# Cross-attention block on one core: the order of the first four blocks laid out anew, with division behind the values and seven-product projection from block 0

## The chip, the core and the metric

The kernel runs on one core of one Trainium2 chip. The metric is device time in microseconds (us), the median of the runs. One further execution is recorded by the hardware profiler; all durations below come from it. The engines are PE (matmul, with its weight loads shown apart as PEld), DVE (vector), ACT (scalar), POOL (GpSimd) and SP (here it only issues transfers).

## The reference

`x` is (16, 1024, 512), the context (16, 64, 512) and the condition (16, 512), all float32. There are 16 heads of 32 features.

```python
def ada_ln(x, c, W_ss, b_ss):            # layer norm, scale and shift from the condition
    h = (x - mean(x)) / sqrt(var(x) + 1e-5)
    scale, bias = split(silu(c) @ W_ss + b_ss, 2)
    return (1 + scale)[:, None, :] * h + bias[:, None, :]

xq, xkv = ada_ln(x, cond, Wss_q, bss_q), ada_ln(ctx, cond, Wss_kv, bss_kv)
q       = xq @ Wq + bq                   # 16 heads x 32
k, v    = split(xkv @ Wkv + bkv)         # 64 keys per batch element
attn    = softmax(q k^T / sqrt(32))      # over the 64 keys
out     = x + (attn v) @ Wp + bp
```

## The kernel before

The 16 x 1024 rows are worked in 32 blocks `i` of 512 rows, so two blocks belong to one batch element; the context is loaded and turned into keys and values for two batch elements at once. All tiles are float32.

One block goes through these steps, named by the helpers that emit them:

- `load_x`; `q_stats` (DVE, row statistics, L260, four tiles); `q_scale` (reciprocal deviation: two small activations on ACT, then small steps on DVE, or, if called "apart", on POOL); `hidden` (ACT normalises four tiles, L321); `turn` (DVE transposes 32 x 32 squares into `ht`); `move` (sixteen transfers from `ht` into `xt`, L508). After these, `xt` holds the features along the partitions.
- The query projection. Blocks 0 to 4 use `queries(i, o)`: four groups of four matmuls of 512 columns (L542), each copied out of PSUM by ACT (`queried`). Blocks 0 to 3 use weights already multiplied with the scale (`query_weights`), later blocks scaled features (`scale_features`, ACT). From block 5 on, `query_product(i, 1..7)` multiplies in seven products instead of eight (Strassen's way, each product four matmuls of 256 columns, L625). It uses sums of weights (`query_weight_sums`, POOL, once) and of features (`feature_sums`, POOL); PSUM banks 0 and 1 collect the products, `query_seed` copies one bank into the other (ACT), `query_out` (ACT) and `query_added` (DVE, L662) take the results out.
- `scores(i, z)` for the two halves `z` of the keys: sixteen matmuls (L673) into two PSUM pair tiles of their own (`ps_s`). DVE takes a maximum over each pair per 32 rows (L685), ACT copies the pair to SBUF (L694). A "crossed" order is maximum 0, copy 1, maximum 1, copy 0; readers of the same tile follow one another. `maxima` merges the two halves and spreads them (DVE, L716), `subtract` takes them off (POOL, L729, two steps; on DVE for block 0), `weights` is the exponential (ACT, L735).
- The softmax denominator goes one of two ways. Blocks 0 to 2 use `sums` (DVE, both halves), `inverse`, and `divide` (POOL, two steps on the 128 x 2048 weights) before `mix`, and `mixed` copies the result out. From block 3 on the division stands behind the values: `total` adds the two halves (POOL, L768), `row_total` sums the rows (DVE), `inverse_rows` takes the reciprocal and sends it through DRAM into another layout (five transfers on SP), `spread_rows` spreads it (DVE), and `divided` multiplies it with the result of `mix` (DVE, L805) on its way out of PSUM.
- `mix` multiplies the weights with the values (L825), into the two pair tiles, or for block 0 into four banks.
- The output projection. Blocks 0 and 1 use `project(i, t)`: four groups of four matmuls of 512 columns (L852), an addition and a transfer out each. From block 2 on `product(i, 1..7)` (L933) does it in seven products, with `weight_sums` (POOL, once), `row_sums` (POOL, two calls of two steps), `biased` (ACT writes the bias into banks 2 and 3), and `added` (DVE, L947). In the `project` way the bias is added to the residual rows beforehand (`residual`, POOL).

The kernel has a manual schedule: each engine carries out its instructions in the order in which the calls stand in the program, and waits at an instruction whose operands aren't ready; what stands behind it waits too. All transfers are issued from SP in this order; a transfer on that queue waits for the eighth before it. PSUM holds the two pair tiles and four single banks, which `bank` hands out in a ring. Blocks 0 to 3 (with the setup: scale and shift rows, biases, `b_v`, `b_p`, weights) have an order written out call by call. From block 4 on a loop over `i` interleaves block `i`'s scores and weights with the projection of blocks `i - 1` and `i - 2`, the queries of `i + 1`, and the way in of `i + 2` to `i + 5`; a tail ends the last two blocks. The call order of a stretch of the way in, for instance, is

```python
    scores(1, 0)
    queries(2, 0)
    q_stats(3)
    queries(2, 1)
    q_scale(3)
    scores(1, 1)
    maxima(1)
    subtract(1)
```

Of the kernel before, what the change touches and what calls it, by code (L numbers as in the profile page):

```python
# [11 lines left out]
ALU = mybir.AluOpType  # L12
# [8 lines left out]
def cross_attention_block(  # L21
# [16 lines left out]
):  # L38

# [99 lines left out]
    def load_x(i):  # L139
        t = xpool.tile([P, NT, H], F32, tag="x", name=f"x_{i}")  # L140
        nc.sync.dma_start(t, rows_of(x, i))
        x_tiles[i] = t
# [34 lines left out]
    for c in range(NC):  # L177
        nc.sync.dma_start(
            b_v_sb[c * 32 : (c + 1) * 32, :],
            b_kv[H + c * P : H + (c + 1) * P].rearrange("(o h) -> o h", o=1).to_broadcast([32, P]),  # L180
        )
# [123 lines left out]
    def q_scale(i, kvb=None):  # L305
        n = NT if kvb is None else NT + 1
        q_rstd[i] = rstd_of(q_mv.pop(i)[:, :n, :], n, "q", i > 1)
        if kvb is not None:
            kv_rstd[kvb] = (q_rstd[i], NT)
# [180 lines left out]
    def turn(i, ts):  # L490

        if ts[0] == 0:
            ht_tiles[i] = hpool.tile([P, 4, NC, NT, 32], F32, tag="ht", name=f"ht_{i}")
        for t in ts:
            nc.vector.transpose(
                ht_tiles[i][:, :, :, t, :].rearrange("p k c b -> p c k b"),
                x_tiles[i][:, t, :].rearrange("p (c k b) -> p c k b", c=NC, k=4),
            )
        if ts[-1] == NT - 1:
            x_tiles.pop(i)  # L500

    def move(i):

        ht = ht_tiles.pop(i)
        xt = qpool.tile([P, 4, NC, NT * 32], F32, tag="xt", name=f"xt_{i}")
        for k in range(4):
            for g in range(4):
                nc.sync.dma_start(  # L508
                    xt[32 * k : 32 * k + 32, g],
                    ht[32 * g : 32 * g + 32, k].rearrange("p c t b -> p c (t b)"),  # L510
                )
        xt_tiles[i] = xt
# [20 lines left out]
    def queries(i, o, later=False):  # L533
        xt, b = xt_tiles[i], i // BPB
        w = wq_tiles.get(b, w_q_sb)
        if o == 0:

            tag = "vb" if i in (1, 3) else "qt"
            qt_tiles[i] = qpool.tile([P, NC, TB], F32, tag=tag, name=f"qt_{i}", bufs=1)
# [13 lines left out]
    def queried(i, o):  # L553
        pq, b = pq_tiles.pop((i, o)), i // BPB
        dst = qt_tiles[i][:, o, :]
# [194 lines left out]
    def inverse(i):  # L750

        v = small.tile([P, HPC * NJ], F32, tag="v", name=f"v_{i}")
        both(v, l_tiles.pop(i), ALU.add)
        nc.vector.reciprocal(v, v)
        vb_tiles[i] = spread(i, v, f"vb_{i}", other=i in (1, NB - 1))
# [9 lines left out]
    def total(i):  # L765

        t = big.tile([P, HPC, TB], F32, tag=f"big{(i + 1) % 2 * 2}", name=f"sum_{i}")
        nc.gpsimd.tensor_tensor(t, s_tiles[i, 0], s_tiles[i, 1], ALU.add)  # L768
        sum_tiles[i] = t

    def row_total(i):
# [7 lines left out]
        )  # L779

# [187 lines left out]
    query_bias_rows()  # L968
    kv_stats(0)
# [10 lines left out]
    load_x(2)  # L980
    load_residual(0)
    load_projection_bias()
# [3 lines left out]
    move(1)  # L986
    load_projection()
    load_x(3)
# [8 lines left out]
    hidden(2, range(NT))  # L997


    scores(0, 0)  # L1000
    turn(2, range(NT))
    move(2)
    load_context(2)
    load_x(4)
    load_residual(1)
    residual(0)
    value_products(0)
    scores(0, 1)
    maxima(0)
    subtract(0, nc.vector, (0,))  # L1010
    value_tiles(0)
    subtract(0, nc.vector, (1,))
    queries(1, 0)
    query_weights(1)
    queries(1, 1)
    weights(0, 0)
    queries(1, 2)
    weights(0, 1)
    sums(0, 0)
    queries(1, 3)  # L1020
    query_weight_sums()
    sums(0, 1)
    inverse(0)
    divide(0)
    scores(1, 0)
    queries(2, 0)
    q_stats(3)
    queries(2, 1)
    q_scale(3)
    scores(1, 1)  # L1030
    maxima(1)
    subtract(1)
    queries(2, 2)
    hidden(3, (0, 1))
    mix(0, apart=False)
    mixed(0)
    hidden(3, (2, 3))
    queries(2, 3)
    turn(3, range(NT))
    move(3)  # L1040
    kv_stats(2)
    q_stats(4)
    project(0, 0)
    weights(1, 0)
    sums(1, 0)
    project(0, 1)
    weights(1, 1)
    residual(1)


    load_x(5)
    q_scale(4)
    kv_scale(2)
    scores(2, 0)
    sums(1, 1)
    inverse(1)
    divide(1)
    project(0, 2)
    context_hidden(2)
    hidden(4, (0, 1))  # L1060
    scores(2, 1)
    maxima(2)
    subtract(2)
    weight_sums()
    hidden(4, (2, 3))
    project(0, 3)
    queries(3, 0)
    queries(3, 1)
    queries(3, 2)
    turn(4, range(NT))  # L1070
    load_residual(2)
    move(4)
    mix(1)
    mixed(1)
    q_stats(5)
    weights(2, 0)
    queries(3, 3)
    project(1, 0)
    sums(2, 0)
    weights(2, 1)  # L1080
    project(1, 1)
    sums(2, 1)
    inverse(2)
    divide(2)
    q_scale(5)
    context_features(2)
    scale_features(4)
    project(1, 2)


    load_x(6)
    scores(3, 0, crossed=True)
    project(1, 3)
    ring[:] = [0, 1]
    scores(3, 1)
    maxima(3)
    subtract(3)
    queries(4, 0)
    load_residual(3)
    hidden(5, (0, 1))  # L1100
    biased(2, 2)
    mix(2)
    mixed(2)
    hidden(5, (2, 3))
    q_stats(6)
    turn(5, range(NT))
    move(5)
    q_scale(6)
    row_sums(2, 0)
    load_x(7)  # L1110
    queries(4, 1)
    product(2, 1)
    added(2, 1)
    product(2, 2)
    weights(3, 0)
    added(2, 2)
    biased(2, 3)
    weights(3, 1)
    total(3)
    queries(4, 2)  # L1120
    keys(2)
    hidden(6, range(NT))
    scale_features(5)
    row_sums(2, 1)
    turn(6, range(NT))
    load_x(8)
    product(2, 7)
    q_stats(7)
    value_products(2)
# [3 lines left out]
    queries(4, 3)  # L1133
    feature_sums(5)
    move(6)
# [198 lines left out]
```

## Time and profile before

| | |
|---|---|
| median of 3 runs | 1057.75 us (1057.16 to 1058.77) |
| profiled execution, its own time | 1058.86 us |
| its span (first to last instruction) | 1057.1 us |
| mean clock granted to PE | 0.998 |
| HBM read / written | 78.85 MB / 34.44 MB |
| page's chain that ended last | PE 80%, DVE 5%, POOL 5%, DMA 4% |

In rows of the page, a group of instructions has the line, the engine, the operation, output and inputs with their shapes, the number of instructions, then "busy us, mean ns of one", and "idle before", the time in which the engine stood still just before them, with what ended it. In a timeline, each row is a run of equal instructions: start, length from the first start to the last end, engine, line and shapes; square brackets hold an idle time ahead of it and what ended that. Busy time is an average over stages with different limits, so the way in is read from timelines and stretches and not from the shares.

### The profile page before, as it was taken

How to read it: one execution, taken by the hardware profiler on the slowest of the kernel's cores; microseconds unless marked ns; L12 is line 12 of the kernel's file. 1: busy time of each engine (PE TensorE's matmuls, PEld its weight loads, DVE VectorE, ACT ScalarE, POOL GpSimd, SP SyncE). 2: the span in 40 equal slices, each digit the busy share in tenths (PEclk: the TensorE clock that was granted, in tenths of full speed). 3: DMA queues.
4: the chain of work that ended last, by engine and by line, in shares of the span. 5: the costliest groups of instructions: out<-in, count | busy, mean ns of one | idle time of the engine just before them, and what ended most of it. 6: DMA issues, size and time to landing. Idle time of an engine off the chain costs nothing.

```text
span 1057.1 us, 22537 instructions
## 1 busy us (share of the span) xinstructions
PE 1033.6 (98%) x8914; PEld 733.7 (69%) x8914; DVE 854.7 (81%) x1134; ACT 618.0 (58%) x951; POOL 752.7 (71%) x470
## 2 busy tenths in 40 slices
PE   6999998999999999999999999999999999999998
PEld 4534365777777787777787787777777777777433
DVE  5698648987789877888878878898778887776993
ACT  3566665665575655667556666566566765565330
POOL 0258794889768869788668986688886886787340
PEclk9999999999999999999999999999999999999999
DMA  9743444444535344544345443444454443334202
GB/s 337 248 127 111 130 122 127 155 150 147 161 94 162 123 140 145 171 148 127 106 131 164 153 158 112 126 141 150 139 157 134 152 134 116 98 115 162 82 30 90
DMA packets 99976, 147.27 MB, mean 139 GB/s; under 512 B 29944, under 2 KB 30096, under 8 KB 99872
## 3 DMA queue, kind: packets, MB, share of 16 engines
q1 hardware_dynamic: 99872, 145.85, 43.5%
q8 instruction: 70, 1.15, 0.5%
q14 instruction: 34, 0.28, 0.1%
HBM read 78.85 MB, written 34.44 MB: 107 GB/s over the span
## 4 chain that ended last, share of the span: by engine, by line
PE 80%; DVE 5%; POOL 5%; DMA 4%; SPq 2%; issue 2%; ACT 1%; POOLq 0%; DVEq 0%; ACTq 0%
PE pp L933 28%; PE pq L625 27%; PE po L825 6%; PE ps L673 6%; PE pp L852 5%; PE pq L542 3%; SPq L508 2%; PE pv L431 2%; PE pk L395 2%; POOL s L760 2%; DMA wss_kv<-in_L_xcond_Wss_kv_dram 2%; DMA b_p_sb<-in_L_xcond_bp_dram 1%; POOL s L729 1%; DMA x<-in_x_dram 1%; DVE s L729 1%
## 5 line engine op out<-in xcount | busy, mean ns | idle before, releaser
L729 POOL TENSOR_TENSOR s<-s,mb 128x2048 f32<-128x2048 f32 x58 | 263.1, 4560 | 160.8 <-DVE mb L716 160.8
L694 ACT COPY s<-ps 128x1024 f32<-128x1024 f32 x128 | 129.5, 1012 | 119.7 <-DVE m L685 82.9
L685 DVE TRANSPOSE_TENSOR_REDUCE m<-ps 128x32 f32<-128x1024 f32 x128 | 150.6, 1214 | 27.1 <-PE ps L673 27.1
L655 ACT ACTIVATE qt<-pq,bias_t 128x256 f32<-128x256 f32 x208 | 85.8, 463 | 110.9 <-PE pq L625 110.9
L933 PE MATMUL pp<-w_p_sb,ot 128*128 128x256 f32 x648 | 148.7, 379 | 0.0
L735 ACT ACTIVATE s<-s 128x2048 f32<-128x2048 f32 x64 | 122.3, 1911 | 42.4 <-POOL s L729 31.8
L947 DVE TENSOR_TENSOR r<-pp,r 128x512 f32<-128x512 f32 x189 | 122.5, 670 | 25.5 <-PE pp L933 19.8
L933 PEld LDWEIGHTS pp<-w_p_sb,ot 128*128 128x128 f32 x648 | 123.4, 190 | 17.4 <-issue 0.7
L768 POOL TENSOR_TENSOR sum<-s,s 128x2048 f32<-128x2048 f32 x27 | 122.7, 4543 | 0.8 <-ACT s L735 0.8
L933 PEld LDWEIGHTS pp<-WT,s 128*128 128x128 f32 x432 | 78.9, 192 | 54.0 <-issue 29.3
L933 PE MATMUL pp<-WT,s 128*128 128x256 f32 x432 | 109.3, 397 | 0.0
L933 PE MATMUL pp<-WT,ot 128*128 128x256 f32 x432 | 102.2, 380 | 0.0
L625 PE MATMUL pq<-xt_sums,wq_sums 128*128 128x256 f32 x416 | 101.0, 386 | 0.0
L321 ACT ACTIVATE x<-x,rstdq 128x512 f32<-128x512 f32 x128 | 96.7, 807 | 4.8 <-POOL rstdq L285 3.2
L625 PE MATMUL pq<-xt,wq_sums 128*128 128x256 f32 x416 | 99.0, 381 | 0.0
L625 PEld LDWEIGHTS pq<-xt_sums,wq_sums 128*128 128x128 f32 x416 | 77.0, 190 | 31.1 <-issue 21.8
L625 PE MATMUL pq<-xt,w_q_sb 128*128 128x256 f32 x416 | 98.4, 380 | 0.1
L260 DVE BATCH_NORM_STATS2 bs<-x 128x6 f32<-128x512 f32 x128 | 86.9, 679 | 5.0 <-DMA x<-in_x_dram 5.0
L662 DVE TENSOR_TENSOR qt<-pq,qt 128x256 f32<-128x256 f32 x104 | 39.1, 418 | 63.1 <-PE pq L625 62.5
L933 PEld LDWEIGHTS pp<-WT,ot 128*128 128x128 f32 x432 | 82.2, 190 | 11.0
L565 ACT ACTIVATE xt<-xt,ss_q 128x512 f32<-128x512 f32 x112 | 84.7, 810 | 6.1 <-DMA xt<-ht 4.3
L625 PEld LDWEIGHTS pq<-xt,w_q_sb 128*128 128x128 f32 x416 | 79.1, 190 | 11.0 <-PE pp L933 0.4
(139 smaller groups left out, 1725.0 us busy)
## 6 DMA issues: line engine op xcount, KB each, us to landing
x<-in_x_dram SPq DMA_DIRECT2D x32, 1024.0 KB, 6.4
r<-in_x_dram SPq DMA_DIRECT2D x32, 1024.0 KB, 5.5
xt<-ht SPq DMA_DIRECT2D x496, 64.0 KB, 2.0
out_dram<-r SPq DMA_DIRECT2D x54, 512.0 KB, 3.8
out_dram<-r SPq DMA_DIRECT2D x20, 256.0 KB, 2.0
wss_q<-in_L_xcond_Wss_q_dram SPq DMA_DIRECT2D x2, 1024.0 KB, 8.8
ctx<-in_ctx_dram SPq DMA_DIRECT2D x8, 256.0 KB, 3.2
wss_kv<-in_L_xcond_Wss_kv_dram SPq DMA_DIRECT2D x2, 1024.0 KB
```

The costliest lines, as they stand in the source:

```text
L260: nc.vector.bn_stats(bs, r)
L321: nc.scalar.activation(dst, src, AF.Identity, bias=rstd[:, 1, j : j + 1], scale=rstd[:, 0, j : j + 1])
L565: nc.scalar.activation(xt[:, :, c, :], xt[:, :, c, :], AF.Identity, scale=ss["q"][:, c, b : b + 1], bias=ss["q"][:, NC + c, b : b + 1],)
L625: nc.tensor.matmul(qa[k][:, m * HT : (m + 1) * HT].rearrange("p (g n) -> p g n", g=2), lhsT=a[:, c, m * P : (m + 1) * P], rhs=x[:, :, c, : ...
L655: nc.scalar.activation(dst, src, AF.Identity, bias=bq_t[:, o : o + 1])
L685: nc.vector.tensor_reduce(m_tiles[i][:, z, 2 * e : 2 * e + 2, :], pss[e].rearrange("p r (j a) -> p r j a", a=32), AX.X, ALU.max, apply_tra ...
L694: nc.scalar.copy(s_sb[:, 2 * e : 2 * e + 2, :], pss[e])
L729: eng.tensor_tensor(s_tiles[i, z], s_tiles[i, z], mb_tiles[i], ALU.subtract)
L735: nc.scalar.activation(p, p, AF.Exp, scale=SCALE)
L768: nc.gpsimd.tensor_tensor(t, s_tiles[i, 0], s_tiles[i, 1], ALU.add)
L933: nc.tensor.matmul(acc[k][:, t * HO : (t + 1) * HO], lhsT=rows[:, c, t * P : (t + 1) * P], rhs=cols[:, c, :], start=n == 2 and t == 0 and ...
L947: nc.vector.tensor_add(r, acc[k].rearrange("p (t h) -> p t h", t=2), r)
```

## The change

Only the order of blocks 0 to 3 and the helpers below change; the loop from block 4 on and the tail are call for call the same.

- Blocks 0 to 2 divide behind the values. Blocks 0 and 2 do it as later blocks do (`total`, `row_total`); block 1 keeps its two `sums` and merges them in the new `halves_total`. The tile of block 0's total lies in the "ot" buffer.
- Blocks 0 and 1 use the seven products for the projection, block 4 for its queries. The residual's bias steps for these blocks go; `biased` takes their place.
- The whole order of blocks 0 to 3 is written anew, with crossed scores throughout.
- `move` issues half of its sixteen transfers from POOL for blocks 1, 2, 3 and 5.
- Large loads are issued at other places: `x` of block 2 ahead of the value bias; `w_p`, `b_p` and the residual rows of block 0 later; `x` of block 3 goes into a residual buffer, `ht` of block 2 into a buffer of the weights.
- `q_scale(2)` does its small steps on DVE.

The helpers:

```diff
     def load_x(i):
-        t = xpool.tile([P, NT, H], F32, tag="x", name=f"x_{i}")
+        t = xpool.tile([P, NT, H], F32, tag="r" if i == 3 else "x", name=f"x_{i}")
         nc.sync.dma_start(t, rows_of(x, i))
         x_tiles[i] = t
...
     nc.sync.dma_start(w_kv_sb, w_kv.rearrange("(c p) o -> p c o", p=P))
     b_v_sb = const.tile([P, P], F32, name="b_v_sb")
-    for c in range(NC):
-        nc.sync.dma_start(
-            b_v_sb[c * 32 : (c + 1) * 32, :],
-            b_kv[H + c * P : H + (c + 1) * P].rearrange("(o h) -> o h", o=1).to_broadcast([32, P]),
-        )
+    def load_value_bias():
+        for c in range(NC):
+            b = b_kv[H + c * P : H + (c + 1) * P].rearrange("(o h) -> o h", o=1)
+            nc.sync.dma_start(b_v_sb[c * 32 : (c + 1) * 32, :], b.to_broadcast([32, P]))
...
     def q_scale(i, kvb=None):
         n = NT if kvb is None else NT + 1
-        q_rstd[i] = rstd_of(q_mv.pop(i)[:, :n, :], n, "q", i > 1)
+        q_rstd[i] = rstd_of(q_mv.pop(i)[:, :n, :], n, "q", i > 2)
...
     def turn(i, ts):
         if ts[0] == 0:
-            ht_tiles[i] = hpool.tile([P, 4, NC, NT, 32], F32, tag="ht", name=f"ht_{i}")
+            pool, tag = (big, "big2") if i == 2 else (hpool, "ht")
+            ht_tiles[i] = pool.tile([P, 4, NC, NT, 32], F32, tag=tag, name=f"ht_{i}")
...
         xt = qpool.tile([P, 4, NC, NT * 32], F32, tag="xt", name=f"xt_{i}")
         for k in range(4):
             for g in range(4):
-                nc.sync.dma_start(
+                (nc.gpsimd if i in (1, 2, 3, 5) and k % 2 else nc.sync).dma_start(
                     xt[32 * k : 32 * k + 32, g],
                     ht[32 * g : 32 * g + 32, k].rearrange("p c t b -> p c (t b)"),
                 )
...
     def queries(i, o, later=False):
         xt, b = xt_tiles[i], i // BPB
         w = wq_tiles.get(b, w_q_sb)
-        if o == 0:
-            tag = "vb" if i in (1, 3) else "qt"
-            qt_tiles[i] = qpool.tile([P, NC, TB], F32, tag=tag, name=f"qt_{i}", bufs=1)
         pq = bank(f"pq_{i}_{o}")
         for c in range(NC):
             nc.tensor.matmul(
...
     def queried(i, o):
         pq, b = pq_tiles.pop((i, o)), i // BPB
+        if o == 0:
+            tag = "vb" if i == 1 else "qt"
+            qt_tiles[i] = qpool.tile([P, NC, TB], F32, tag=tag, name=f"qt_{i}", bufs=1)
...
         v = small.tile([P, HPC * NJ], F32, tag="v", name=f"v_{i}")
         both(v, l_tiles.pop(i), ALU.add)
         nc.vector.reciprocal(v, v)
-        vb_tiles[i] = spread(i, v, f"vb_{i}", other=i in (1, NB - 1))
+        vb_tiles[i] = spread(i, v, f"vb_{i}", other=i == NB - 1)
...
     def total(i):
-        t = big.tile([P, HPC, TB], F32, tag=f"big{(i + 1) % 2 * 2}", name=f"sum_{i}")
+        if i == 0:
+            t = opool.tile([P, HPC, TB], F32, tag="ot", name="sum_0")
+        else:
+            t = big.tile([P, HPC, TB], F32, tag=f"big{(i + 1) % 2 * 2}", name=f"sum_{i}")
         nc.gpsimd.tensor_tensor(t, s_tiles[i, 0], s_tiles[i, 1], ALU.add)
         sum_tiles[i] = t
...
+    def halves_total(i):
+        lt_tiles[i] = small.tile([P, HPC, NJ], F32, tag="lt", name=f"lt_{i}")
+        both(lt_tiles[i].rearrange("p r j -> p (r j)"), l_tiles.pop(i), ALU.add)
```

The order, from the first queries to the loop (`+` new, `-` before):

```diff
     first_features((3,))
     query_weights(0)
     query_bias_rows()
+    load_x(2)
+    load_value_bias()
     kv_stats(0)
     kv_scale(0)
     queries(0, 0, later=True)
...
     hidden(1, (0, 1))
     queries(0, 1)
     hidden(1, (2, 3))
-    load_x(2)
-    load_residual(0)
-    load_projection_bias()
     for h in range(2):
         scale_shift_rows("kv", h)
     turn(1, range(NT))
     move(1)
+    load_x(3)
     load_projection()
-    load_x(3)
+    load_projection_bias()
     queries(0, 2)
     for h in range(2):
         scale_shift("kv", 2 * NC, h)
...
     queries(0, 3)
     keys(0)
     hidden(2, range(NT))
-    scores(0, 0)
     turn(2, range(NT))
     move(2)
+    load_x(4)
+    load_residual(0)
     load_context(2)
-    load_x(4)
-    load_residual(1)
-    residual(0)
     value_products(0)
+    value_tiles(0)
+    scores(0, 0, crossed=True)
+    q_stats(3, (0, 1, 2))
+    queries(1, 0)
     scores(0, 1)
     maxima(0)
-    subtract(0, nc.vector, (0,))
-    value_tiles(0)
-    subtract(0, nc.vector, (1,))
-    queries(1, 0)
+    subtract(0, nc.vector)
+    queries(1, 1)
     query_weights(1)
-    queries(1, 1)
+    weight_sums()
+    queries(1, 2)
     weights(0, 0)
-    queries(1, 2)
+    q_stats(3, (3,))
+    q_scale(3)
+    queries(1, 3)
     weights(0, 1)
-    sums(0, 0)
-    queries(1, 3)
-    query_weight_sums()
-    sums(0, 1)
-    inverse(0)
-    divide(0)
-    scores(1, 0)
+    total(0)
+    ring[:] = [0, 1]
+    scores(1, 0, crossed=True)
+    hidden(3, (0, 1))
     queries(2, 0)
-    q_stats(3)
-    queries(2, 1)
-    q_scale(3)
+    hidden(3, (2, 3))
+    turn(3, range(NT))
+    move(3)
+    row_total(0)
+    inverse_rows(0)
+    load_x(5)
+    load_residual(1)
     scores(1, 1)
     maxima(1)
     subtract(1)
+    queries(2, 1)
     queries(2, 2)
-    hidden(3, (0, 1))
-    mix(0, apart=False)
-    mixed(0)
-    hidden(3, (2, 3))
+    biased(0, 2)
+    mix(0)
+    spread_rows(0)
+    divided(0)
     queries(2, 3)
-    turn(3, range(NT))
-    move(3)
-    kv_stats(2)
-    q_stats(4)
-    project(0, 0)
     weights(1, 0)
+    queries(3, 0, later=True)
+    row_sums(0, 0)
+    q_stats(4, (0, 1))
     sums(1, 0)
-    project(0, 1)
+    q_stats(4, (2, 3), kvb=2)
     weights(1, 1)
-    residual(1)
-    load_x(5)
-    q_scale(4)
-    kv_scale(2)
-    scores(2, 0)
-    sums(1, 1)
-    inverse(1)
-    divide(1)
-    project(0, 2)
-    context_hidden(2)
+    product(0, 1)
+    added(0, 1)
+    product(0, 2)
+    added(0, 2)
+    row_sums(0, 1)
+    q_scale(4, kvb=2)
+    query_weight_sums()
+    biased(0, 3)
+    scores(2, 0, crossed=True)
+    queries(3, 1, later=True)
+    scores(2, 1)
     hidden(4, (0, 1))
-    scores(2, 1)
+    queried(3, 0)
+    hidden(4, (2, 3))
+    queried(3, 1)
     maxima(2)
     subtract(2)
-    weight_sums()
-    hidden(4, (2, 3))
-    project(0, 3)
-    queries(3, 0)
-    queries(3, 1)
+    product(0, 7)
+    added(0, 7)
+    product(0, 6)
+    added(0, 6)
     queries(3, 2)
+    sums(1, 1)
+    halves_total(1)
+    inverse_rows(1)
+    product(0, 5)
+    added(0, 5)
     turn(4, range(NT))
+    move(4)
+    load_x(6)
+    product(0, 4)
+    added(0, 4)
+    product(0, 3)
+    added(0, 3)
     load_residual(2)
-    move(4)
+    weights(2, 0)
+    biased(1, 2)
     mix(1)
-    mixed(1)
     q_stats(5)
-    weights(2, 0)
+    spread_rows(1)
+    divided(1)
+    context_hidden(2)
     queries(3, 3)
-    project(1, 0)
-    sums(2, 0)
+    q_scale(5)
     weights(2, 1)
-    project(1, 1)
-    sums(2, 1)
-    inverse(2)
-    divide(2)
-    q_scale(5)
+    total(2)
+    row_sums(1, 0)
     context_features(2)
+    product(1, 1)
+    added(1, 1)
+    product(1, 2)
+    added(1, 2)
+    row_sums(1, 1)
+    biased(1, 3)
+    row_total(2)
+    inverse_rows(2)
     scale_features(4)
-    project(1, 2)
-    load_x(6)
     scores(3, 0, crossed=True)
-    project(1, 3)
-    ring[:] = [0, 1]
+    feature_sums(4)
+    product(1, 7)
+    product(1, 6)
+    added(1, 7)
+    added(1, 6)
     scores(3, 1)
+    hidden(5, (0, 1, 2))
     maxima(3)
     subtract(3)
-    queries(4, 0)
+    query_product(4, 1)
+    query_seed(4)
+    product(1, 5)
+    added(1, 5)
+    query_product(4, 2)
+    query_out(4, 2)
+    product(1, 4)
+    product(1, 3)
+    hidden(5, (3,))
+    spread_rows(2)
+    added(1, 4)
+    added(1, 3)
+    biased(2, 2)
     load_residual(3)
-    hidden(5, (0, 1))
-    biased(2, 2)
     mix(2)
-    mixed(2)
-    hidden(5, (2, 3))
-    q_stats(6)
+    divided(2)
+    row_sums(2, 0)
     turn(5, range(NT))
     move(5)
-    q_scale(6)
-    row_sums(2, 0)
     load_x(7)
-    queries(4, 1)
+    query_product(4, 6)
+    weights(3, 0)
+    query_out(4, 6)
     product(2, 1)
+    q_stats(6, (0, 1))
     added(2, 1)
     product(2, 2)
-    weights(3, 0)
+    q_stats(6, (2, 3))
     added(2, 2)
-    biased(2, 3)
+    q_scale(6)
     weights(3, 1)
     total(3)
-    queries(4, 2)
-    keys(2)
+    query_product(4, 7)
+    query_out(4, 7)
+    biased(2, 3)
+    row_sums(2, 1)
+    key_products(2, spare("pk_2"))
     hidden(6, range(NT))
+    query_product(4, 5)
+    query_added(4, 5)
+    key_tiles(2)
+    query_product(4, 4)
+    query_added(4, 4)
     scale_features(5)
-    row_sums(2, 1)
     turn(6, range(NT))
     load_x(8)
-    product(2, 7)
-    q_stats(7)
-    value_products(2)
+    value_products(2, spare("pv_2"))
     value_tiles(2)
     row_total(3)
     inverse_rows(3)
-    queries(4, 3)
+    query_product(4, 3)
+    query_out(4, 3)
     feature_sums(5)
+    product(2, 7)
+    q_stats(7)
     move(6)
     q_scale(7)
```

## Prediction

> **What bounds the kernel now.** I read the page's busy shares first, then the stretches around the way in (blocks 0 to 3, written out by hand) and the first turn of the loop (block 4).
>
> ```profile
> PE 1033.6 (98%) x8914; PEld 733.7 (69%) x8914; DVE 854.7 (81%) x1134; ACT 618.0 (58%) x951; POOL 752.7 (71%) x470
> 165.00:170.00 5.00, 2.83 (x12) 1.85 (x11) 4.95 (x7) 2.32 (x7) 2.46 (x6) 1.00 0.15 50
> 170.00:175.00 5.00, 4.16 (x39) 2.71 (x40) 4.42 (x5) 2.83 (x4) 0.00 (x0) 0.68 0.23 46
> ```
>
> The columns of the last two are the stretch, its length, busy time of PE, PEld, DVE, ACT, POOL, then PE's granted clock and DMA. PE is the bound; the one hole with a lower clock (0.68) lies in block 4. PE's timeline there, and at the projections:
>
> ```profile
> 82.60 7.03 PE L852 MATMUL pp<-w_p_sb,ot 128*128 128x512 f32 x16
> 89.56 1.14 PE L673 MATMUL ps<-qt,kt 32*32 32x512 f32 x32
> 142.27 3.62 PE L933 MATMUL pp<-w_p_sb,ot 128*128 128x256 f32 x16
> 161.96 1.98 PE L673 MATMUL ps<-qt,kt 32*32 32x512 f32 x32
> 165.94 1.97 PE L625 MATMUL pq<-xt,w_q_sb 128*128 128x256 f32 x8
> 170.84 1.25 PE L673 MATMUL ps<-qt,kt 32*32 32x512 f32 x32 [2.94 <-ACT s L694]
> 172.02 3.56 PE L933 MATMUL pp<-WT,s 128*128 128x256 f32 x8
> 175.42 1.89 PE L933 MATMUL pp<-w_p_sb,ot 128*128 128x256 f32 x8
> 196.98 1.14 PE L673 MATMUL ps<-qt,kt 32*32 32x512 f32 x32
> 226.61 1.14 PE L673 MATMUL ps<-qt,kt 32*32 32x512 f32 x32
> ```
>
> The first number is the start. Eight fp32 matmuls of 512 columns (a quarter of a block's projection) go start to start in 3.44 to 3.64, eight of 256 (a product) in 1.73 to 1.83. Block 4 takes 196.98 - 161.96 = 35.0; block 5 takes 29.6, 0.4 of them context transposes. So block 4 loses 5.8: an idle of 2.94, a product at half speed after it (3.40 start to start for 1.73), and small waits. The other prices:
>
> ```profile
> L729 POOL TENSOR_TENSOR s<-s,mb 128x2048 f32<-128x2048 f32 x58 | 263.1, 4560 | 160.8 <-DVE mb L716 160.8
> L694 ACT COPY s<-ps 128x1024 f32<-128x1024 f32 x128 | 129.5, 1012 | 119.7 <-DVE m L685 82.9
> L735 ACT ACTIVATE s<-s 128x2048 f32<-128x2048 f32 x64 | 122.3, 1911 | 42.4 <-POOL s L729 31.8
> L768 POOL TENSOR_TENSOR sum<-s,s 128x2048 f32<-128x2048 f32 x27 | 122.7, 4543 | 0.8 <-ACT s L735 0.8
> xt<-ht SPq DMA_DIRECT2D x496, 64.0 KB, 2.0
> ```
>
> The last says that each of a block's sixteen transfers into xt lands 2.0 after its issue; the trace gives 0.51/0.59/2.00 (least, median, most) for the issue itself.
>
> **Removed: work.** Eight projections (from 82.60, 90.63, 95.34, 115.08, 122.39 and 126.98) take 28.2 on PE; fourteen products take 14 x 1.75 = 24.5: -3.7. Block 4's four query groups (3.63 + 3.54 + 3.43 + 3.63 = 14.2) become seven products (12.3): -2.0. Together -5.7. POOL and DVE lose divisions and second row sums (block 0 alone: 9.0 on POOL, 4.5 on DVE) and gain a total (4.5), half sums (5.1) and a division (2.4); neither sets the end by its sum.
>
> **Removed: waits.** From 18.1 to 161.96 PE loses 0.78 (keys' tile), 0.97 (xt of block 1), 1.09 and 0.35 (scores of block 1), 1.93 (mix of block 0, which fills four banks), 0.60, 0.43 and 0.3: 6.4. Block 4 loses 5.8. If nothing new waited, the change would gain 5.7 + 6.4 + 5.8 = 17.9.
>
> **Added: waits.** The new order of each engine is walked with the rows' durations. ACT's fixed costs: a query copy 0.67, a chain of row statistics 1.15, a hidden tile 0.73. DVE's: a maximum 1.2, a spread 2.31, statistics 0.8 a tile. PE's own walk, in starts: values 38.7, scores(0,0) 42.4, queries(1,0) 43.4, scores(0,1) 47.1, three query groups 48.15 to 58.55; scores(1,0) 60.3, queries(2,0) 61.4, scores(1,1) 65.0, two groups 66.1 to 73.2, mix(0) to 76.45, two groups to 83.4, two products, scores(2,0) and queries(3,1) to 91.65; scores(2,1) 93.2, two products to 97.75; queries(3,2) 99.25, three products, mix(1) 108.1, queries(3,3) 110.4, transposes to 114.4; two products from 115.75, scores(3,0) to 120.35; product(1,7) 124.85. From there the steps follow with the waits below to scores(4,0) at 165.85. What PE waits for:
> - scores(1,0) for the last query copy of block 1. It stands on ACT behind q_scale(3), which needs the fourth tile's statistics, and DVE has these behind both subtractions: maxima (from 48.15) 2.35, merge 0.3, spread 2.3, subtractions 4.6, statistics 0.8, so 58.5; ACT then 1.15 and 0.67, 60.3. PE comes at 58.55. Wait 1.75.
> - mix(0) needs the score banks, whose maxima stand behind row_total(0) on DVE: ends 76.45, 0.95 late.
> - scores(2,1): DVE does five statistics tiles, a row sum, two additions and a maximum after divided(0), and ACT a bias copy and two copies: banks free 10.2 after it (93.2), PE there at 91.65. Wait 1.55.
> - queries(3,2): bank 0 is held until the copy of queries(3,0), on ACT behind four hidden tiles' first half and the copies of scores(2,1): 99.25 against 97.75. Wait 1.5.
> - product(1,1): divided(1) stands on DVE behind q_stats(5) (3.2) and spread_rows(1) (2.3): 115.75 against 114.4. Wait 1.35.
> - product(1,7): row_sums(1,0) stands on POOL behind total(2), that needs weights(2,1), that stands on ACT behind q_scale(5) and the last query copy of block 3. From the end of queries(3,3): 0.1 + 0.67 + 1.15 + 1.9 + 4.55 + 2.6 = 11.0; PE has 6.5 of work and waiting until then. Wait 4.5, the largest.
> - query_product(4,2): its seed copy stands on ACT behind the copies of scores(3,1) and three hidden tiles, 6.9 after the scores start; PE comes at 4.6. Wait 2.3.
> - scores(4,1): statistics of block 7 (3.2) stand on DVE ahead of the maxima, behind values' tiles, row_total(3) and reciprocal. Counting from the end of the values: banks free at 10.1, PE there at 8.05. Wait 2.05.
>
> These make 15.95. Nothing is charged for steps that are moved under cover: query_weight_sums (four by 1.27) now stands on POOL ahead of subtract(2), done at 97.1 where the spread for it ends at 98.8, so 1.7 of cover; weight_sums falls into POOL's idle stretch near 46 to 52; the four halves of added() are DVE steps of 0.65 counted above. Then the clock: in the trace a hole of 2.94 is followed by 3.4 at half speed, a loss of 1.67. The wait of 4.5 is longer, so I add 1.7; the two near 2 get nothing, since the trace's holes of 0.9 and less cost nothing (between: 0 to 1.7 each, nearer the small ones in place of work; kept for the range). Sum 17.65.
>
> [...]
>
> **Added: moves on two queues.** Half of the transfers into xt of blocks 1, 2, 3 and 5 are issued from POOL, which issues none now. Bounds for one: 0.2 (POOL's smallest instruction, L283) and 2.0 (SP's slowest). I take SP's median row, 0.6, the same transfer. Up to about 1.0 it costs nothing: block 1's last must issue by 41.4 (turned at 31.2, so 1.28 each); block 3's by 77.9 (turned at 68.6: 1.17) and before subtract(1) at 76.3 (0.96); block 5's ahead of q_scale(6) (1.0). On SP a transfer waits for the eighth before it, so large loads now stand behind moves: xt of block 1 is there near 41.2 instead of 46.5. That wait is among the 6.4. x of block 3 takes a free residual buffer, issued near 37, landing 6.4 later (43.4), before DVE reads it at 45.75 (2.3 of cover). w_p, b_p and r_0 come later than now, but well before weight_sums (46) and added(0,1) (89). The row transfers of inverse_rows(0) stand on SP behind eight moves to 73.7, and land at 78.2; DVE waits for them, 1.9 behind its spread for block 1, and this is in the walk: mix(0) and two query groups keep PE at work until 83.4, divided(0) ends at 83.0.
>
> [...]
>
> **Sum.** 1058.86 (profiled execution; span 1057.1 and 1.8 around it) - 5.7 - 6.4 - 5.8 + 17.65 = 1058.6. The profiled execution lies 1.1 above the median of the runs, so the median becomes 1057.5. The walk itself gives scores(4,1) at 172.4, where before has 170.84 and then 1.67 of clock, 172.5: the two ways agree. Behind block 4 the orders are equal. About 0.2% (2.1 us) is what a measurement can tell from no change.
>
> **Rivals.**
> *Same* (0.36): gain and new waits cancel, 1057.5.
> *Faster* (0.32): the waits for score banks and for what follows the copies (1.55, 1.5, 2.3, 2.05) each count one copy of 1.01 on ACT that may already be done when the maximum ends: -4.0, so 1053.4. For it: in the loop the first copy of a crossed pair starts with the maximum. Against: copies wait 82.9 for maxima over the kernel. If the clock does not drop either, 1051.8.
> *Slower* (0.32): the issue on POOL. A block has eight of these in a row, so at 1.35 each block 1 is 0.55 late, block 3 1.45, block 5 1.9 (2.8 less what PE waits for anyway), +3.9, so 1061.4. It decides from about 1.2 on. At 2.0 it would be 5.8, 6.7 and 7: 1077. For it: one engine must do both issue and arithmetic. Against: SP's same transfers at 0.6.
> That the products are not fewer is no rival: the new PE order shows them.
>
> **Range.** From 1051.8 (the faster case without the clock's drop) to 1063.8 (1.45 each on POOL: 0.8 more in each of three blocks than at 1.35). The likeliest case's own range is 1055.4 to 1059.6. The chances: faster by over 0.2% 0.32, within 0.36, slower 0.32.
>
> **What would show it.** Right: PE idle of some 4 to 5 before the third product of block 1, and PEclk under 1 there; no such hole left in block 4 (a wait of 2); scores(4,0) starting near 165.9 where it starts at 161.96 now, and scores(5,0) at 197 in both. POOL's DMA rows under 1.0. Wrong: scores(5,0) before 194 or after 200; a wait of PE on xt; a hole in PE that is not in the list.

## The result and the profile after

| | before | after |
|---|---|---|
| median, 11 runs each | 1058.11 us (1056.57 to 1060.41) | 1062.20 us (1060.36 to 1065.70) |
| ratio | | 1.0037, 95% interval 1.0025 to 1.0049 |
| profiled execution (span) | 1058.86 (1057.1) | 1060.41 (1058.2) |

The kernel became slower by 4.1 us, where no change was forecast. In the listing after, product is L945, scores L677, query products L629, the copies of scores L698, `subtract` L733, `total` L776 and the moves L512; in the later versions lines stand a few further down. The page's busy shares, then stretches with the columns of the prediction (PEclk is the last but two):

```profile
PE 1028.0 (97%) x8986; PEld 745.8 (70%) x8986; DVE 862.9 (82%) x1150; ACT 613.0 (58%) x944; POOL 754.6 (71%) x494
125.00:130.00 5.00, 3.43 (x10) 2.79 (x11) 4.47 (x5) 2.60 (x3) 4.84 (x5) 0.74 0.83 303
170.00:175.00 5.00, 3.63 (x24) 2.85 (x31) 3.95 (x7) 3.14 (x8) 1.85 (x5) 1.00 0.18 35
```

PE is busy for 5.6 us less (4.6 of it ahead of block 5's first scores, 1.0 behind them, where the orders are equal), and the span is longer all the same. The stretch with a lowered clock has moved from block 4 (0.68 at 170) to the third product of block 1 (0.74 at 125). PE's timeline (start, length, engine and line, in brackets the idle time ahead) shows every wait that the prediction listed:

```profile
61.07 1.13 PE L677 MATMUL ps<-qt,kt 32*32 32x512 f32 x26 [0.85 <-ACT qt L564]
73.90 3.19 PE L837 MATMUL po<-s,vt 32*32 32x512 f32 x64
...
94.31 1.47 PE L677 MATMUL ps<-qt,kt 32*32 32x512 f32 x32 [2.01 <-ACT s L698]
...
100.98 3.70 PE L542 MATMUL pq<-xt,wq 128*128 128x512 f32 x8 [1.55 <-ACT qt L564]
...
117.63 3.72 PE L945 MATMUL pp<-w_p_sb,ot 128*128 128x256 f32 x16 [1.42 <-DVE ot L817]
...
126.57 2.99 PE L945 MATMUL pp<-WT,ot 128*128 128x256 f32 x8 [4.15 <-POOL ot L921]
129.35 2.62 PE L945 MATMUL pp<-WT,s 128*128 128x256 f32 x8
131.91 1.14 PE L677 MATMUL ps<-qt,kt 32*32 32x512 f32 x32
...
139.18 1.99 PE L629 MATMUL pq<-xt,w_q_sb 128*128 128x256 f32 x8 [2.48 <-ACT pq L641]
...
168.56 1.22 PE L677 MATMUL ps<-qt,kt 32*32 32x512 f32 x32
174.80 1.46 PE L677 MATMUL ps<-qt,kt 32*32 32x512 f32 x32 [1.37 <-ACT s L698]
199.59 1.14 PE L677 MATMUL ps<-qt,kt 32*32 32x512 f32 x32
```

The first scores of block 5 start at 199.59 where they started at 196.98. From there the orders are equal, and the difference shrinks to 1.3 by 976, in steps of 0.1 to 0.5 in single blocks: one execution against one other is no more exact than that. The wait of 4.15 is as the prediction had it. POOL's timeline there:

```profile
119.41 4.54 POOL L776 TENSOR_TENSOR sum<-s,s 128x2048 f32<-128x2048 f32 x1 [0.86 <-ACT s L739]
123.89 1.28 POOL L920 TENSOR_TENSOR s<-ot 128x512 f32<-128x512 f32 x1
125.25 1.27 POOL L921 TENSOR_TENSOR ot<-ot 128x512 f32<-128x512 f32 x1
```

The rows that product (1,7) needs were divided on DVE by 118.7 (116.35 and 2.36):

```profile
116.35 2.36 DVE L817 TENSOR_TENSOR ot<-po,vb 128x1024 f32<-128x1024 f32 x2
```

POOL takes them up at 123.89, behind the total of block 2.

The runs also list the clock granted over the whole span. One stretch of half speed costs 1.7 of 1058, which is 0.0016 of it, so 0.998 stands for one, 0.997 for two, 0.995 for three. The profiles, read in stretches of 2 us, bear this out: the clock that they lose is 1.7 us here, and 3.4, 5.1 and 11.9 in other versions, which is one, two, three and seven such stretches. Of 21 runs of the kernel before, beside four of the experiments, 19 have 0.998, one 0.999, one 1.000 (beside the last two, on another chip, five of eleven have 1.000, so how often it comes differs). Of the 11 after, three have 0.998, four 0.997, four 0.992 to 0.995. The three at 0.998 took 1060.36 to 1060.94; the 19 before at 0.998 have a median of 1058.19. So of the 4.1, about 2.2 is there at equal clock, and 1.8 goes with further half speed, which the profiled execution happened not to have.

### The profile page after: what moved, and what is told of

Its sections match the earlier page's. It is cut to its first block, busy times and chain, and to the rows that moved or that the text cites. A ratio compares the mean times of both kernels' runs of the same rounds, so it can differ in the third digit from the quotient of the medians.

```text
span 1058.2 us, 22778 instructions
## 1 busy us (share of the span) xinstructions
PE 1028.0 (97%) x8986; PEld 745.8 (70%) x8986; DVE 862.9 (82%) x1150; ACT 613.0 (58%) x944; POOL 754.6 (71%) x494
## 4 chain that ended last, share of the span: by engine, by line
PE 85%; DVE 6%; ACT 3%; DMA 3%; POOL 2%; issue 1%; SPq 0%; ACTq 0%; DVEq 0%; POOLq 0%
PE pp L945 32%; PE pq L629 30%; PE po L837 6%; PE ps L677 6%; PE pp L864 3%; PE pv L434 3%; PE pq L542 3%; PE pk L398 3%; DMA wss_kv<-in_L_xcond_Wss_kv_dram 2%; DVE m L689 2%; DVE s L733 1%; POOL sum L776 1%; DVE bs L263 1%; ACT s L698 1%; DVE lt L781 1%
## 5 line engine op out<-in xcount | busy, mean ns | idle before, releaser
L733 POOL TENSOR_TENSOR s<-s,mb 128x2048 f32<-128x2048 f32 x58 | 263.1, 4560 | 164.2 <-DVE mb L720 161.0
L698 ACT COPY s<-ps 128x1024 f32<-128x1024 f32 x128 | 129.2, 1012 | 114.9 <-DVE m L689 77.3
L945 PE MATMUL pp<-w_p_sb,ot 128*128 128x256 f32 x696 | 159.8, 379 | 1.4 <-DVE ot L817 1.4
L959 DVE TENSOR_TENSOR r<-pp,r 128x512 f32<-128x512 f32 x203 | 131.9, 670 | 32.5 <-PE pp L945 25.0
L945 PEld LDWEIGHTS pp<-w_p_sb,ot 128*128 128x128 f32 x696 | 132.2, 190 | 20.4 <-DVE ot L817 1.7
L776 POOL TENSOR_TENSOR sum<-s,s 128x2048 f32<-128x2048 f32 x29 | 131.7, 4541 | 3.1 <-ACT s L739 3.1
L945 PEld LDWEIGHTS pp<-WT,s 128*128 128x128 f32 x464 | 84.4, 191 | 55.3 <-issue 30.4
L945 PE MATMUL pp<-WT,s 128*128 128x256 f32 x464 | 116.0, 393 | 0.0
L945 PE MATMUL pp<-WT,ot 128*128 128x256 f32 x464 | 110.8, 382 | 4.2 <-POOL ot L921 4.2
L629 PE MATMUL pq<-xt_sums,wq_sums 128*128 128x256 f32 x432 | 104.9, 386 | 0.0
L629 PE MATMUL pq<-xt,w_q_sb 128*128 128x256 f32 x432 | 102.3, 379 | 2.5 <-ACT pq L641 2.5
L629 PE MATMUL pq<-xt,wq_sums 128*128 128x256 f32 x432 | 102.8, 381 | 0.0
L629 PEld LDWEIGHTS pq<-xt_sums,wq_sums 128*128 128x128 f32 x432 | 79.8, 190 | 32.4 <-issue 22.6
L945 PEld LDWEIGHTS pp<-WT,ot 128*128 128x128 f32 x464 | 88.5, 191 | 18.0 <-POOL ot L921 5.1
L629 PEld LDWEIGHTS pq<-xt,w_q_sb 128*128 128x128 f32 x432 | 81.9, 190 | 14.8 <-ACT pq L641 2.9
L629 PEld LDWEIGHTS pq<-xt,wq_sums 128*128 128x128 f32 x432 | 80.5, 190 | 11.5 <-issue 1.2
```

Source lines behind the costliest of these rows:

```text
L629: nc.tensor.matmul(qa[k][:, m * HT : (m + 1) * HT].rearrange("p (g n) -> p g n", g=2), lhsT=a[:, c, m * P : (m + 1) * P], rhs=x[:, :, c, : ...
L698: nc.scalar.copy(s_sb[:, 2 * e : 2 * e + 2, :], pss[e])
L733: eng.tensor_tensor(s_tiles[i, z], s_tiles[i, z], mb_tiles[i], ALU.subtract)
L945: nc.tensor.matmul(acc[k][:, t * HO : (t + 1) * HO], lhsT=rows[:, c, t * P : (t + 1) * P], rhs=cols[:, c, :], start=n == 2 and t == 0 and ...
L959: nc.vector.tensor_add(r, acc[k].rearrange("p (t h) -> p t h", t=2), r)
```

## The experiments

Two theories were set against each other: the waits of the new order gave the gain back (the prediction's walk), or the loss came from elsewhere (POOL's transfers, the chip's clock). The runs come from three chips, each with runs of the kernel before beside them: a median of 1058.15 before for the first two experiments below, the moves on SP and the first version with the waits taken up; 1058.28 for the four matmuls and the second such version; 1057.57 for the last two. Between chips the ratios are compared.

**The largest wait.** One engine is exchanged:

```diff
-    total(2)
+    total(2, nc.vector)
```

> One edit on the changed kernel: the total of block 2 is added on DVE (about 2.3 us there) and not on POOL (4.54). Theory 1 (the waits that the new order adds give the gain back, the largest of them 4.15 us ahead of the third product of block 1, with 1.8 us of half clock behind it, because row_sums(1,0) stands behind total(2) on POOL): that hole goes, a wait of about 2 for the banks of scores(3,0) appears, because row_total(2) still stands ahead of the maxima, scores(4,0) starts near 164.0 where it starts at 168.56, and the median falls by 4 to 5 us, to 0.9995 of the kernel before. Theory 2 (the 4 us more come from elsewhere, from POOL's transfers or from the later part): the median stays within 1 us of the changed kernel's, 1.003 to 1.004.

Measured: 1058.72 us, ratio 1.0011 (1.0002 to 1.0020), 3.5 us under the changed kernel. PE's timeline:

```profile
125.00 1.97 PE L945 MATMUL pp<-WT,ot 128*128 128x256 f32 x8 [1.68 <-ACT pp L908]
...
166.43 1.22 PE L677 MATMUL ps<-qt,kt 32*32 32x512 f32 x32
```

The 4.15 went, 1.68 for a bias copy (unforeseen) and 0.88 for the score banks (2 expected) came, and scores(4,0) starts 2.1 earlier, not 4.5. In this execution the wait of 2.14 at scores(2,1), which had cost no clock before, did (the granted clock is 0.50 in the 2 us from 96). Three of the eleven runs have a clock of 1.000 (1057.2 to 1057.6). This holds with the first theory; its size, 4 to 5, was too large.

**PE kept busy in the hole.** Matmuls that nobody reads stand behind scores(3,0), in a bank that is free there:

```diff
     scores(3, 0, crossed=True)
+    pd = bank("dummy", 1)
+    for _ in range(9):
+        nc.tensor.matmul(pd, lhsT=w_p_sb[:, 0, :P], rhs=w_p_sb[:, 0, :], start=True, stop=True)
```

> One edit on the changed kernel: nine matmuls of 512 columns (about 3.96 us), whose result nobody reads, fill the 4.15 us hole ahead of the third product of block 1. The wait stays, PE is not idle in it. Theory 1 with the clock (the half-speed stretch behind the hole costs 1.8 us in the profile, and a drop of this kind that comes in some executions and not in others is why the median lies 1.8 above the profiled execution): products (1,7) and (1,6) take 3.6 us and not 5.4, scores(4,0) starts 1.8 earlier, at 166.8, and the clocks of the timed runs gather at 0.997 to 0.999; the median falls by 2 to 3 us, to 1.0015 of before. Theory 2 (the clock is a matter of the chip's state and not of this hole): the half speed turns up elsewhere, the median stays at 1.0035 to 1.004.

Measured: 1065.56 us, ratio 1.0065 (1.0052 to 1.0078). Nine of them took 7.99 us, as a timeline row counts two entries for each (eight entries are four matmuls, in the rows of the prediction too), and filled twice the hole. So it tells nothing on the median, though product (1,7) behind it ran at full speed; in this execution half speed followed the holes of 2.31 and 2.49 at scores(2,1) and query_product(4,2) instead. It was repeated with `range(4)`:

> The changed kernel with four idle-filling matmuls of 512 columns in the hole ahead of the third product of block 1, now sized by the run before (nine took 7.99 us, so 0.89 each, and held PE up by 3.7): 3.55 us in a hole of 4.15, whose result nobody reads. Theory 1 (a hole of more than some 2 us lets the clock fall to one half for some 3.5 us, in some executions and not in others, which costs 1.7 to 2 us each time; the changed kernel has three such holes, 2.0, 4.15 and 2.5, where the kernel before has one, 2.94): the two products behind the hole run at full speed, one place for a drop is gone and two are left, granted clocks of the runs are 0.998 and 0.997 and seldom under, the median falls by 1 to 2 us from 1062.2, to 1060.2 to 1061.2, 1.002 to 1.003 of before. Theory 2 (the clock falls whatever PE does): the median stays within 0.5 of 1062.2.

Measured: 1060.52 us, ratio 1.0027 (1.0016 to 1.0037), 1.7 under the changed kernel, or 1.1 by the ratios, whose intervals overlap; five of eight clocks are 0.998, the others 0.997, 0.996, 0.995. This is what the first theory expected, but the size is not clear of noise: the wait is still there, and only the clock behind it was mended. PE's timeline in that version:

```profile
122.36 3.70 PE L1127 MATMUL dummy<-w_p_sb 128*128 128x512 f32 x8
126.60 1.99 PE L945 MATMUL pp<-WT,ot 128*128 128x256 f32 x8 [0.53 <-POOL ot L921]
...
137.52 3.45 PE L629 MATMUL pq<-xt,w_q_sb 128*128 128x256 f32 x8 [2.48 <-ACT pq L641]
```

Product (1,7) takes 1.99 where it took 2.99, but here the hole of 2.48 is followed by half speed (3.45 for 1.99), which the same hole was not in the changed kernel's execution, and so is one of 2.54 at scores(2,1). That filling one hole leaves fewer stretches in a run rests on the eight clocks alone.

**All moves on SP.**

```diff
-                (nc.gpsimd if i in (1, 2, 3, 5) and k % 2 else nc.sync).dma_start(
+                nc.sync.dma_start(
```

> One part undone on the changed kernel: all transfers into xt are issued from SP again, none from POOL. Theory 1 (an issue on POOL takes 0.5 us, costs PE nothing and takes load off SP): sixteen on SP take 10 to 12.7 us; xt of block 1 lands near 45.7, so PE waits 1.7 at 43.9; the five transfers of inverse_rows(0) move behind eight more issues, about 4.9 us, so divided(0) ends near 89 and the first product of block 0 waits 5 us, with a clock drop likely behind it: 5 to 8 us slower than the changed kernel, 1.008 to 1.011 of before. Theory 2 (the slower rival of the forecast, issue on POOL is what made it slower): 2 to 4 us faster than the changed kernel, 1.000 to 1.002.

Measured: 1074.67 us, ratio 1.0162 (1.0149 to 1.0175), 12.5 slower than the changed kernel, more than the 5 to 8 expected. The clocks of its four runs are 0.988 to 0.990; its profile loses 11.9 us of clock, seven stretches, where the changed kernel's median run has two. Five more are up to 8.6 of the 12.5 (a part of them falls into the holes themselves), so much of the loss is the clock behind longer holes and not the waits alone. SP's, DVE's and PE's timelines:

```profile
31.49 12.22 SPq L512 DMA_DIRECT2D xt<-ht  x16
```

```profile
49.45 0.69 DVE L263 BATCH_NORM_STATS2 bs<-x 128x6 f32<-128x512 f32 x1 [3.05 <-DMA x<-in_x_dram]
...
91.31 2.31 DVE L807 STREAM_TRANSPOSE vb<-vr 128x2048 f32<-128x2048 f32 x1 [8.35 <-DMA vr<-ltd]
```

```profile
65.71 2.00 PE L677 MATMUL ps<-qt,kt 32*32 32x512 f32 x26 [4.03 <-ACT qt L564]
```

The 8.35 at the rows of `inverse_rows(0)` was foreseen (PE then waits 3.42 for the first product of block 0, where 5 was expected). The 3.05 was not: x of block 3 is issued behind the sixteen moves, its statistics stand on DVE ahead of the maxima, and scores(1,0) then waits 4.03. Issue on POOL, in the changed kernel's own timeline, takes 0.5 each (the median of all 32 is 0.50):

```profile
31.38 4.11 POOL L512 DMA_DIRECT2D xt<-ht  x8 [30.07 <-DVE ht L499]
```

So this part of the change is a gain, and the forecast's slower rival is wrong.

**The waits taken up.** The steps that stood ahead of each wait were moved. The core of the edit (the total of block 2 also gets a tile in the spread buffer, since its old one is needed by scores(3,0)):

```diff
-    q_scale(3)
     queries(1, 3)
+    q_scale(3)
...
     scores(2, 0, crossed=True)
+    biased(0, 3)
+    sums(1, 1)
+    halves_total(1)
+    inverse_rows(1)
     queries(3, 1, later=True)
-    scores(2, 1)
-    hidden(4, (0, 1))
+    scores(2, 1, crossed=True)
     queried(3, 0)
...
-    q_stats(5)
-    spread_rows(1)
     divided(1)
...
+    q_stats(5)
     weights(2, 1)
-    total(2)
     row_sums(1, 0)
...
     row_sums(1, 1)
+    total(2)
...
+    query_product(4, 1)
+    query_seed(4)
     scores(3, 1)
```

> The changed kernel with each of its waits taken up by moving the step that stood ahead: the last query copy of block 1 ahead of q_scale(3); sums and inverse of block 1, maxima of scores(2,0) and the two additions ahead of the second half of block 4's statistics; query copies of block 3 ahead of the hidden tiles; q_stats(5) behind divided(1); row_sums(1,0) and (1,1) ahead of total(2), whose tile lies in the spread buffer; copies of scores(3,0) ahead of half of scale_features(4); query_product(4,1) and its seed ahead of scores(3,1); half of block 7's statistics earlier. Block 4's moves are half on POOL too. Theory 1 (these waits are the whole of it): waits of 0.85, 2.0, 1.5, 1.4, 4.15 with 1.8 of clock, 2.5 and 1.4 go for the most part, scores(4,0) starts at 156 to 160, and the time is 1052 to 1055, 0.994 to 0.997 of before. Theory 2 (DVE and ACT are full there, and what is moved turns up as another wait): scores(4,0) at 164 or later, 1.000 or above.

Measured: 1054.51 us, ratio 0.9972 (0.9962 to 0.9983): faster than before and within the 1052 to 1055 expected, but scores(4,0) starts only at 163.41, not at 156 to 160. The profiled execution is the slowest of the ten runs (1058.28, clock 0.994), so it shows more half speed than the median run, whose clock is 0.998. PE's timeline, then POOL's:

```profile
117.24 1.12 PE L351 MATMUL pkt<-ident,hk 128*128 128x128 f32 x4 [3.61 <-ACT hk L324]
118.15 6.00 PE L948 MATMUL pp<-w_p_sb,ot 128*128 128x256 f32 x16
...
170.50 2.33 PE L677 MATMUL ps<-qt,kt 32*32 32x512 f32 x32 [2.06 <-ACT s L698]
```

```profile
101.16 9.05 POOL L733 TENSOR_TENSOR s<-s,mb 128x2048 f32<-128x2048 f32 x2 [4.56 <-DVE mb L720]
110.16 0.20 POOL L285 TENSOR_TENSOR workq<-workq 128x5 f32<-128x5 f32 x1
```

The old holes went and two new ones of over 2 us came. The hidden tile of the context was late because q_scale(4), moved later, has its small steps on POOL behind both halves of subtract(2) (110.16). The next version put these steps on DVE, q_stats(7) and q_scale(7) ahead of turn(6), and a query copy ahead of the last copy of scores(2,1), where `between` is called:

```diff
-        q_rstd[i] = rstd_of(q_mv.pop(i)[:, :n, :], n, "q", i > 2)
+        q_rstd[i] = rstd_of(q_mv.pop(i)[:, :n, :], n, "q", i > 2 and i != 4)
...
-    scores(2, 1, crossed=True)
-    queried(3, 0)
+    scores(2, 1, crossed=True, between=lambda: queried(3, 0))
...
-    q_stats(7, (0, 1))
+    q_stats(7)
     scale_features(5)
+    q_scale(7)
```

> The version with the waits taken up, its new waits taken up in turn: small steps of q_scale(4) on DVE (on POOL they stood behind subtract(2), 4.6 us, which held hidden(4), turn(4), divided(1) and the context's hidden tile, a hole of 3.61 and 2.4 of half clock); the context's hidden tile right behind hidden(4); the query copy (3,0) ahead of the last copy of scores(2,1) (a hole of 1.03); all of q_stats(7) and q_scale(7) ahead of the transposes of block 6 (a hole of 2.06 and 2.0 of half clock at scores(4,1)). Theory 1 (these are the waits that are left): scores(4,0) starts at 157 to 158 where it started at 163.4, the loop follows without the hole in its first turn, and the time is 1046 to 1050, 0.989 to 0.992 of before, with the granted clock at 0.999 or 1.000 in most runs. Theory 2 (DVE, 0.9 busy there, is the bound now): a new hole of 3 us or more, 1052 or above.

Measured: 1056.94 us, ratio 0.9989 (0.9980 to 0.9998), slower than the version before it (by 0.0017 in the ratio, with intervals that overlap at their ends), where 1046 to 1050 was expected. DVE's timeline, POOL's, and PE's:

```profile
104.06 4.42 DVE L292 SCALAR_TENSOR_TENSOR workq<-mvq,workq 128x5 f32<-128x5 f32 x1
```

```profile
99.48 8.98 POOL L735 TENSOR_TENSOR s<-s,mb 128x2048 f32<-128x2048 f32 x2 [4.38 <-DVE mb L722]
```

```profile
109.54 3.78 PE L950 MATMUL pp<-WT,ot 128*128 128x256 f32 x8 [5.25 <-DVE r L964]
```

A DVE step on five numbers a row, 0.17 us elsewhere, took 4.42 and ended with POOL's second subtract (104.06 and 4.42 are 108.48, 99.48 and 8.98 are 108.46). An addition stood behind it on DVE, and PE waited 5.25 for that. The last version puts the small steps on POOL between the two halves of the subtract:

```diff
-    subtract(2)
+    subtract(2, zs=(0,))
...
     q_scale(4, kvb=2)
+    subtract(2, zs=(1,))
...
     divided(1)
+    weights(2, 1)
     queries(3, 3)
     q_stats(5)
-    weights(2, 1)
...
     query_out(4, 3)
+    q_scale(7)
     feature_sums(5)
```

> The version before with three places mended. (1) The small steps of q_scale(4) go back to POOL, between the two halves of subtract(2): on DVE one of them, 128 x 5 elements, took 4.42 us (others of its kind 0.17 to 0.42) and ended when POOL's subtract did, at 108.46, so the addition behind it held the last product of block 0 for 5.25. [...] (2) both exponentials of block 2 ahead of the last query copy of block 3; (3) q_scale(7) behind the last query copy of block 4 (0.47). Expected: scores(4,0) at 156 to 158 where it was 164.1, 1047 to 1051, 0.990 to 0.994 of before. Theory 2 (the 4.42 was a mischance of one execution and DVE's load is the bound): 1054 or above.

Measured: 1049.23 us, ratio 0.9925 (0.9913 to 0.9936), 8.3 us under the kernel before on that chip (1057.57) and some 13 under the changed one. PE's timeline:

```profile
137.35 3.69 PE L950 MATMUL pp<-w_p_sb,ot 128*128 128x256 f32 x16 [0.93 <-DVE ot L822]
...
157.57 1.76 PE L677 MATMUL ps<-qt,kt 32*32 32x512 f32 x32
```

From block 0's scores on no bracketed wait of PE is over 0.93 before the loop, scores(4,0) starts at 157.57 where it started at 168.56, and the clock is 1.000 in four of five runs, 0.999 in the other. The small steps take 0.20 each on POOL there, and the hole of 5.25 is gone, so DVE's load was not the bound. Of the kernel before, five of the eleven runs beside it have 1.000 too, with a median of 1056.58, against 1049.58 of the four here: 7.0 at equal clock. The gain is about half of the 17.9 that the prediction reckoned with if nothing new waited. Of the other half, some 1 us are products that were sized too small; PE's rows show many small waits as well, the largest at mix(0), 1.5 (0.55 idle, then 3.27 start to start for 2.28).

**One part undone in that version.** Block 4's queries go back to four groups:

```diff
-    query_product(4, 1)
-    query_seed(4)
     scores(3, 1)
+    queries(4, 0)
...
-    query_product(4, 2)
-    query_out(4, 2)
+    queries(4, 1)
```

> The same with one part of the change undone: block 4's queries in four groups of four matmuls of 512 columns (14.2 us on PE) and not in seven products (12.3). If PE's work is what is left to bound this stretch (theory 1), it is 1.5 to 2.5 us slower than the run above, as the forecast's sum had it (2.0). If another engine bounds it (theory 2), they agree within 0.7, or it is the faster of the two, since the seed copy and the feature sums go.

Measured: 1051.16 us, ratio 0.9940 (0.9923 to 0.9956), 1.9 more than with the products. The number is the one expected from PE's work, but the runs do not show that cause. The intervals of the two ratios overlap, and the difference goes with the clock: three of the six runs have 0.996 to 0.998 and took 1052.19 to 1054.12; the three at 0.999 or 1.000 took 1048.86 to 1050.14, as the five with the products did (1048.54 to 1050.45, all at 0.999 or 1.000). PE's timeline:

```profile
157.27 1.09 PE L677 MATMUL ps<-qt,kt 32*32 32x512 f32 x16
159.60 1.36 PE L677 MATMUL ps<-qt,kt 32*32 32x512 f32 x16 [1.25 <-DVE vt L447]
160.90 3.37 PE L950 MATMUL pp<-WT,s 128*128 128x256 f32 x8
```

scores(4,0) starts at 157.27, no later than with the products. Then PE waits 1.25 for the DVE step that takes the values out of PSUM (158.74), behind the transposes of block 6, and half speed follows (3.37 for 1.99). So what the products of block 4 save is not seen in the time: at equal clock the medians are 1049.97 (three runs) and 1049.23 (five), 0.7 apart, nearer to the second theory than to the 1.5 to 2.5 of the first.

## Why the prediction was right or wrong

**The waits were right in sum,** and singly within 0.7. By its own list, predicted and measured: scores(1,0) 1.75 and 1.9 (0.85 in brackets, and the six matmuls before it spread over 1.05); mix(0) 0.95 and 0.84 (3.12 start to start where other mixes take 2.28); scores(2,1) 1.55 and 2.01; queries(3,2) 1.5 and 1.55; product(1,1) 1.35 and 1.42; product(1,7) 4.5 and 4.15; query_product(4,2) 2.3 and 2.48; scores(4,1) 2.05 and 1.37. Together 15.95 and 15.7. The clock behind the largest was put at 1.7 and cost 1.8 (126.57 to 131.91 for 3.55 of work).

**The term "removed: work" was too large.** Twelve undisturbed products of blocks 0 and 1 take 21.4, so 1.78 each and not 1.75: a product behind another kind of matmul takes 1.83, only one behind a product 1.73. Fourteen save 3.3, not 3.7. Block 4's seven, most of them alone among other work, take 12.9, not 12.3, and save 1.3. Of 5.7 us, 4.6 came. (Among the removed waits, the two at the scores of block 1 are 1.01 and 0.28 from start to start, 2.08 and 1.35 for 1.07, not 1.09 and 0.35.)

**Small things left out.** Values start at 39.24, not 38.7; in the nine profiles with the new order they start between 38.55 and 40.13, so a part is chance. Scores that waited for banks take 1.39 to 1.40 start to start instead of 1.07, twice. With 1.1 from the products these make 2.3 of the 2.6 by which scores(5,0) came later than forecast; the rest was not traced.

**The step that failed most is the last one, from the execution to the median.** The forecast took the median to lie 1.1 under the profiled execution, as in the kernel before (0.75 over its eleven runs); it lies 1.8 above. The changed kernel has three holes over 2 us where the one before has one, each may set off half speed, and this differs from run to run (clocks of 0.992 to 0.998). Its profiled execution had one such stretch; its median run, by its clock of 0.997, has two. That is 2.9 of the 4.7 us between 1057.5 and 1062.2; the other 1.8 lie in the execution itself, 1060.41 where the sum gave 1058.6. The sentence "the two near 2 get nothing" failed here: in the profiled execution they got nothing, in other runs they did.

**The rivals.** The slower one named the wrong mechanism: POOL's issue takes 0.50 (at most 0.69 in 32, beside DVE's statistics, maxima, row sums and additions), under the 1.0 from which it would matter by the prediction's slack, and without it the kernel is 12.5 slower. That its 1061.4 lies near the 1062.2 measured is luck. The faster one did not come: the copies did stand behind the maxima.

## What to carry to other kernels

A new order that removes work gains only if what stands ahead of each step on its own engine is moved as well: here the same parts gave 1.0037 and, with some forty lines of the order moved, 0.9925. Read for each PE wait which engine released it, and what that engine did just before; that is the step to move, and in two of three versions it made the next hole elsewhere. Where a change adds idle times of 2 us or more to PE, count each as a possible stretch of half speed (15 of the 18 counted below were followed by one), and compare medians with the clock of every run beside them.

## What was not expected of the hardware

- PE's idle times between 60 and 202 us in all ten profiles: of twelve between 1.3 and 1.7 us none was followed by half speed, of eleven between 2.0 and 2.54 eight were, of seven of 2.94 and more all. These are counts and no threshold: one of 1.25 was followed by it too, in the version with one part undone. In the profiles before and after, the stretch of half speed lasted 3.4 us each time (a granted clock of 0.50 from 171.8 to 175.2, and from 127.4 to 130.8), a loss of 1.7 of clock; behind the holes of 3.42, 3.61, 4.03 and 5.25 two followed on each other (behind the 5.25, the clock is 0.69, 0.50, 0.50 and 0.60 in the four stretches of 2 us from 106).
- A DVE step with two SBUF inputs, on 128 x 5 numbers, lasted until a POOL step of 4.5 us had ended (4.42 against 0.17 elsewhere). The kernel before has such a row near its end: a subtract on DVE, also with two SBUF inputs, that started at 1013.70, while POOL divided (until 1017.06), took 5.52 against 2.28 elsewhere, and the changed kernel's profile has one of 5.20 at the same place.
